# Adding the two experts' outputs of a node in one DRAM row, with the gates made earlier, in a graph layer with a top-2 mixture of experts

## The chip, the cores and the metric

The kernel runs on one core of a Trainium2 chip, in float32, as a single launch. The metric is the device time in microseconds (us) of that launch, the median of several runs.

## The reference

A graph convolution, a mixture of 64 experts of which each node uses two, a batch norm over all nodes, and a residual with a layer norm. There are N = 12,500 nodes of D = 256 values, and 212,500 edges, sorted by destination; H = 512 and CAP = 1024.

```python
h = feats * rsqrt(deg_out)[:, None]
m = segment_sum(h[src], dst) * rsqrt(deg_in)[:, None]
x = (m @ W_gc + b_gc) + (feats @ W_res + b_res)

logits = x @ Wg + bg                       # [N, 64]
vals, idx = top_k(logits, 2)
gates = softmax(vals, axis=-1)             # two gates per node, their sum is 1
# each expert e: h1 = gelu(rows @ w1[e] + b1[e]); out = h1 @ w2[e] + b2[e]
core = zeros(N, D).at[tok].add(gate * out) # the two outputs of a node, weighted
y = x + core
y = (y - mean(y, 0)) * rsqrt(var(y, 0) + 1e-5) * gamma + beta
result = layernorm(feats + y)
```

## The kernel before

P = 128 is the partition count; the nodes are NT = 98 tiles of 128 (the last one short), NP = 98 x 128 = 12,544. E = 64 experts have RPE blocks of 128 slots each, NSLOT in all. `V`, `S`, `T`, `GP` and `nc.sync` are VectorE (DVE), ScalarE (ACT), TensorE (PE), GpSimd (POOL) and SyncE (SP). The stages follow each other in time.

**Degree count.** Degrees of sources are counted by DVE while `h_d` (the scaled features) is made. Beside it SP writes zeros to all of `z_d`, in pieces of 256 KB.

**Edge and node stage.** `row(c)` gathers 128 source rows from `h_d` with an indirect DMA on POOL (L729) into a ring of 6 x 4 rows and multiplies them on PE with a one-hot matrix of their destinations; 1584 such rows are worked through. The order of all instructions here is written out by hand (`manual_schedule`): each step of the side work calls `later(t, f)`, which puts the next step LAG = 11 rows further on, and the loop over `c` takes the steps that are due. So one engine's step and the next engine's step that needs its result lie 11 rows apart. `own` issues 118 loads of 64 KB on SP here. When all edges of a pair of node tiles are summed, `nodes(t0, n, t)` runs for that pair: `square_root` (ACT) and `scales` for the degree, `scale`, `turn_x`, `turned`, `dense` (x and the 64 logits into one accumulation), then `best`: DVE adds the bias, takes the two largest logits and their places, SP writes the x rows to `x2_d` (L951), DVE keeps the difference of the two logits in `less` (L956), and `keep` copies x to `acc2`, which stays in SBUF. `count`, `ranks`, `codes`, `entries` and `enter` number each node's place within its two experts and enter it in the table `tab` by products on PE. The last three groups of tiles have no edges left beside them, so their chains run one after the other: the tail.

**Slot table.** `tab` holds per slot P * (1 + tile of the node) + row, with P * NT more for a second choice, or 0 where the slot is free. A few DVE operations (L1149 to L1164) turn it into `slot[:, 0]`, the row of `x2_d` to gather, and `slot[:, 1]`, the row of `z_d` to write: first choices to rows 0 to NP - 1, second choices to NP and on, free slots outside of it.

**Experts.** The 64 experts are taken in the order of their counts, largest first, in parts of up to four blocks (`parts`, 83 of them, 241 blocks, 28,352 slots for 25,000 rows). For each part in turn the program has `hidden` (PE and Gelu on ACT), `begin` of the part three further on (for a new expert: its table columns, and 1 MB of weights by SP, L1217 to L1219, three buffers; then `gather`, one indirect DMA per block on POOL, L1229, 16 buffers `xg`), `turn` of the next part (PE transposes and a DVE copy), and `outputs`: per block four products into `yp`, L1278 on DVE adds the bias into `yo` (six buffers), and L1279 scatters 128 rows to `z_d` on POOL. All those scatters are declared free of dependences among each other (group "places"), since each row is given once.

**End, first pass.** The gates are made from `less` (an Exp). For each of twelve loads of eight tiles, and some short ones, SP loads both halves of `z_d` (L1387, 1 MB each, two buffers of both), ACT multiplies the second choices by their gate, tile by tile (L1390), DVE multiplies the first choices and adds them to `acc2`, tile by tile (L1394), and one DVE addition per load adds the second ones (L1399). PE then transposes each tile (L1410), DVE takes the batch norm's statistics from PSUM (L1415), and ACT copies the transposed tiles back (L1417).

**End, second pass.** The batch norm is applied, x is added, and the layer norm is made and written, load by load. The x loads stand behind the z loads on SP.

Of the kernel before, what the change touches and what calls it, by code (L numbers as in the profile page):

```python
# [8 lines left out]
F32 = mybir.dt.float32  # L9
F16 = mybir.dt.float16  # L10
BF16 = mybir.dt.bfloat16
I32 = mybir.dt.int32
# [7 lines left out]
P = 128  # L20
# [81 lines left out]
def gnn_moe_kernel(  # L102
# [25 lines left out]
    x2_d = dram.tile([N, D], F32, name="x2_d")  # L128
    late_d = dram.tile([P, LATE], F32, name="late_d")
    z_d = dram.tile([2 * NP, D], F32, name="z_d")  # L130
# [55 lines left out]
    less = const.tile([P, NT], F32)  # L186
    V.memset(less, 0.0)

# [29 lines left out]
    tables = route.tile([P, 2, 2, NSLOT], I32)  # L218
    slot, sorted_ = tables[:, 0], tables[:, 1]
# [35 lines left out]
    with ExitStack() as stack:  # L255
# [23 lines left out]
        zeros = [(z_all[a], zero) for a in range(NT)]  # L279
# [356 lines left out]
    with ExitStack() as stack:  # L636
# [234 lines left out]
        def nodes(t0, n, t):  # L871
# [67 lines left out]
            def best(t):  # L939
                y, top, i8 = v["y"], v["top"], v["i8"]  # L940
                for i in range(n):
                    V.scalar_tensor_tensor(
                        y[:r, i], gps[i][:r], r_in[:r, t0 + i : t0 + i + 1], bias[:r],
                        op0=ALU.mult, op1=ALU.add,
                    )
                give("gp", t)
                for i in range(n):
                    V.max(top[:r, i], y[:r, i, D:])
                for i in range(n):
                    V.max_index(i8[:r, i], top[:r, i], y[:r, i, D:])  # L950
                nc.sync.dma_start(  # L951
                    x2_d[t0 * P : t0 * P + (n - 1) * P + r].rearrange("(t p) d -> p t d", p=r),
                    y[:r, :n, :D],
                )
                later(t, keep)
                V.tensor_sub(less[:r, t0 : t0 + n], top[:r, :n, 1], top[:r, :n, 0])  # L956
                ix = of("ix", [P, 2, 2])
                V.tensor_copy(ix[:r, :n], i8[:r, :n, 0:2])
                o1 = of("o1", [P, 2, E], BF16)
                both = of("both", [P, 2, E], BF16)  # L960
                for j in range(n):
                    V.tensor_scalar(
                        o1[:r, j], lane_b[:r, :E], ix[:r, j, 0:1], None, op0=ALU.is_equal
                    )
                    V.scalar_tensor_tensor(
                        both[:r, j], lane_b[:r, :E], ix[:r, j, 1:2], o1[:r, j],
                        op0=ALU.is_equal, op1=ALU.add,
                    )
                of("rk", [P, 2, 2])
                take("pp", t, count)  # L970

# [156 lines left out]
        with tc.manual_schedule(engines={  # L1128
# [20 lines left out]
        code = one.tile([P, NSLOT], F32)  # L1149
        V.tensor_copy(code, tab)  # L1150
        second = one.tile([P, NSLOT], F32)
        V.tensor_single_scalar(second, code, P * (NT + 1) - 0.5, op=ALU.is_gt)
        free = one.tile([P, NSLOT], F32)
        V.tensor_scalar(free, code, 0.0, OUTSIDE, op0=ALU.is_equal, op1=ALU.mult)
        node = one.tile([P, NSLOT], F32)
        V.scalar_tensor_tensor(
            node, second, float(-NP), code, op0=ALU.mult, op1=ALU.add
        )
        V.tensor_scalar(node, node, float(-P), 0.0, op0=ALU.add, op1=ALU.max)
        V.tensor_copy(slot[:, 0], node)  # L1160
        V.tensor_add(node, node, free)
        V.scalar_tensor_tensor(
            slot[:, 1], second, float(NP), node, op0=ALU.mult, op1=ALU.add
        )  # L1164
# [44 lines left out]
    with ExitStack() as stack:  # L1209
        wp = stack.enter_context(tc.tile_pool(name="w", bufs=3))  # L1210
        two = stack.enter_context(tc.tile_pool(name="x_two", bufs=2))
# [12 lines left out]
        def gather(at, n):  # L1224

            xg = []
            for k in range(n):
                g = two.tile([P, D], F32, name="xg", bufs=16)
                GP.indirect_dma_start(  # L1229
                    out=g,  # L1230
                    out_offset=None,
                    in_=x2_d,
                    in_offset=bass.IndirectOffsetOnAxis(ap=at[:, 0, k : k + 1], axis=0),
                )
                xg.append(g)
            return xg
# [30 lines left out]
        def outputs(w, bb, at, h1, m, group):  # L1267
            w2 = w[:, 2 * H : 2 * H + 4 * D].rearrange("p (c d) -> p c d", d=D)
            for k in range(-(-m // P)):
                r = min(P, m - k * P)  # L1270
                yp = ps2.tile([P, D], F32, name="yp")
                for j in range(4):
# [5 lines left out]
                V.tensor_add(yo[:r], yp[:r], bb[:r])  # L1278
                st = GP.indirect_dma_start(  # L1279
# [6 lines left out]
                    bounds_check=2 * NP - 1,  # L1286
                    oob_is_err=False,
                )
                if group:
                    tc.declare_no_dep(st.ins, group=group, reason="each row is given once")  # L1290
                    tc.add_to_no_dep_group(group, st.ins)
# [14 lines left out]
        def begin(q):  # L1306
            i, b, m = parts[q]
            if b == 0:
# [20 lines left out]
                )  # L1329
                given[i] = load(regs[i % REGS])  # L1330
# [5 lines left out]

        for q in range(AHEAD):
            begin(q)
        xT = turn(xg.pop(0))
        for q, (i, b, m) in enumerate(parts):  # L1340
            h1 = hidden(given[i][0], xT, m)
            if q + AHEAD < len(parts):
                begin(q + AHEAD)
            if q + 1 < len(parts):
                xT = turn(xg.pop(q + 1))
            outputs(*given[i], table(q), h1, m, "places")


        with tc.If(nc.values_load(over_n[0:1, 0:1]) > 0):
            with tc.For_i(0, E, 1) as e:  # L1350
                w, bb = load(e)
                at = two.tile([P, 2, RPE], I32, name="at")
                V.tensor_copy(at, slot[:, :, bass.ds(e * RPE, RPE)])
                for b in range(0, RPE, 4):
                    ab = at[:, :, b : b + 4]
                    outputs(w, bb, ab, hidden(w, turn(gather(ab, 4)), 4 * P), 4 * P, None)


    with ExitStack() as stack:
# [4 lines left out]
        zq = zq_stack.enter_context(tc.tile_pool(name="f_z", bufs=2))  # L1364
# [9 lines left out]
        gate = one.tile([P, 2, NT], F32)  # L1374
        S.activation(gate[:, 1], less, AF.Exp)
        V.tensor_scalar_add(gate[:, 0], gate[:, 1], 1.0)
        V.reciprocal(gate[:, 0], gate[:, 0])
        V.tensor_mul(gate[:, 1], gate[:, 1], gate[:, 0])


        stat = one.tile([P, 2, 25, 6], F32)
        z3 = [z_d[k * NP : (k + 1) * NP].rearrange("(t p) d -> p t d", p=P) for k in range(2)]
        for t0, n in LOADS:
            r = rows(t0)
            zt = zq.tile([P, 2, 8, D], F32, name="zt")
            for k in range(2):
                nc.sync.dma_start(zt[:r, k, :n], z3[k][:r, t0 : t0 + n])  # L1387
            for i in range(n):
                t = t0 + i
                S.activation(  # L1390
                    zt[:r, 1, i], zt[:r, 1, i], AF.Copy, scale=gate[:r, 1, t : t + 1]
                )
                y = acc2[:r, :, t * P : (t + 1) * P]
                V.scalar_tensor_tensor(  # L1394
                    y, zt[:r, 0, i].rearrange("p (h d) -> p h d", h=2),
                    gate[:r, 0, t : t + 1], y, op0=ALU.mult, op1=ALU.add,
                )
            y = acc2[:r, :, t0 * P : (t0 + n) * P].rearrange("p h (t d) -> p t h d", d=P)
            V.tensor_add(y, y, zt[:r, 1, :n].rearrange("p t (h d) -> p t h d", h=2))  # L1399
# [133 lines left out]
```

## Time and profile before

| | |
|---|---|
| median of three runs | 3382.77 us (3381.10 to 3382.91) |
| the profiled execution | 3381.99 us, span 3380.1 us |
| degree count | 0 to 260 us |
| edge and node stage | 260 to 2242 us |
| its tail and the slot table | 2242 to 2312 us |
| experts | 2312 to 3168 us |
| first pass of the end | 3168 to 3285 us |
| second pass | 3285 to 3380 us |

The stages are read off the trace: where the gathers of the edges begin and end, where PE begins to be busy without a break, where the first load of `z_d` is issued, where the last statistic is done. In the lines of the profile a group is named by its line in the kernel (L729), its engine, its operation, the tiles "out<-in", and its count; then come the busy time, the mean duration of one in ns, and the idle time of the engine just before them with what ended most of it ("<-DMA zt<-z_d": a transfer). "issue" is idle time in which the engine waited for nothing that the profile shows. The granted clock is the share of TensorE's full clock that was granted.

### The profile page before, as it was taken

The numbers are of one execution on the slowest core, as the hardware profiler recorded it, in microseconds if no ns is written. First come the engines' busy times: TensorE is split into PE (matmuls) and PEld (weight loads), VectorE is DVE, ScalarE is ACT, GpSimd is POOL, SyncE is SP. The second block draws the span as 40 slices with busy tenths as digits, with TensorE's granted clock in tenths as the row PEclk, the third lists the DMA queues.
The fourth block names the chain that finished last, engine by engine and source line by source line (L and its number), as shares of the span: only waits on it lengthen the run. The fifth ranks groups of instructions, "written<-read, shape, count | busy, mean of one in ns | idle before, by whom it ended". The sixth has DMA issues, their size and how long they took to land. (4 is left out here: it accounts for less than half of the span.)

```text
span 3380.1 us, 37103 instructions
## 1 busy us (share of the span) xinstructions
PE 2658.2 (79%) x11121; PEld 1756.8 (52%) x11121; DVE 1620.7 (48%) x6071; ACT 732.6 (22%) x2054; POOL 2001.5 (59%) x2088
## 2 busy tenths in 40 slices
PE   5828777777787777777778777867999999999644
PEld 4613344444454444444444444544777766778533
DVE  9986334545545544544454455653122222222498
ACT  8960100000011000010000101111222211222368
POOL 0027777777777777777777777735555555554100
PEclk8866778988878888998888898978999999999865
DMA  9553444444444444444444444423334444556667
GB/s 351 191 165 105 154 118 127 130 125 123 128 130 126 125 127 125 127 129 122 126 125 129 128 124 130 133 73 128 123 121 137 138 146 157 182 179 198 222 217 242
DMA packets 256999, 497.38 MB, mean 147 GB/s; under 512 B 44571, under 2 KB 168985, under 8 KB 248474
## 3 DMA queue, kind: packets, MB, share of 16 engines
q0 software_dynamic: 98800, 264.95, 27.1%
q1 hardware_dynamic: 144696, 217.20, 19.5%
q10 hardware_dynamic: 13298, 12.80, 1.3%
q8 instruction: 91, 1.49, 0.2%
q14 instruction: 114, 0.93, 0.1%
HBM read 401.41 MB, written 96.79 MB: 147 GB/s over the span
## 5 line engine op out<-in xcount | busy, mean ns | idle before, releaser
L729 POOL DMA_INDIRECT ring<-h_d,src_col x1584 | 1511.0, 954 | 495.3 <-issue 425.3
L743 PE MATMUL p<-ring,o 128*128 128x258 f32 x3168 | 1179.6, 482 | 481.8 <-DMA ring<-h_d,src_col 400.1
L743 PEld LDWEIGHTS p<-ring,o 128*128 128x128 f32 x3168 | 603.5, 222 | 976.5 <-DMA ring<-h_d,src_col 647.2
L721 DVE TENSOR_SCALAR o<-lane,rel 128x128 f32<-128x128 f32 x1584 | 384.3, 302 | 591.5 <-PE p L743 591.3
L1273 PE MATMUL yp<-w,h 128*128 128x256 f32 (+3 forms) x1928 | 432.9, 380 | 0.0
L1229 POOL DMA_INDIRECT xg<-x_d,tables x241 | 233.0, 967 | 335.8 <-PE xtp L1244 219.3
L1257 PE MATMUL hp<-xT,w 128*128 128x384 f32 (+11 forms) x1328 | 399.5, 454 | 1.4 <-DVE xT L1248 1.4
L1273 PEld LDWEIGHTS yp<-w,h 128*128 128x128 f32 (+3 forms) x1928 | 341.9, 182 | 64.4 <-issue 7.3
L1261 ACT ACTIVATE h<-hp,w 128x384 f32<-128x384 f32 (+11 forms) x332 | 180.9, 545 | 670.0 <-PE hp L1257 669.1
L776 ACT COPY s<-p 128x258 f32<-128x258 f32 x132 | 49.3, 373 | 1241.6 <-PE p L743 1241.5
L1257 PEld LDWEIGHTS hp<-xT,w 128*128 128x128 f32 x1328 | 248.4, 191 | 131.2 <-issue 56.9
L1279 POOL DMA_INDIRECT z_d<-yo,tables x241 | 238.1, 988 | 121.9 <-DVE yo L1278 65.0
L1248 DVE COPY xT<-xtp 128x768 f32<-128x768 f32 (+2 forms) x83 | 77.4, 932 | 405.6 <-PE xtp L1244 405.6
L1278 DVE TENSOR_TENSOR yo<-yp,bb 128x256 f32<-128x256 f32 (+3 forms) x241 | 102.1, 423 | 276.2 <-PE yp L1273 270.7
L435 ACT ACTIVATE s_lo<-lane_b,nb 128x128 bf16<-128x128 bf16 x581 | 171.0, 387 | 4.4 <-DVE lo_end L426 1.8
L1043 PE MATMUL tab<-at,vals 128*128 128x512 bf16 x392 | 139.7, 447 | 11.6 <-DVE vals L1031 11.6
L583 POOL MEMSET acc<- 128x1792 f32 x10 | 17.5, 1754 | 213.7 <-DMA h_d<-acc 213.7
L928 PE MATMUL bank<-wcat,acc 128*128 128x320 f32 x392 | 137.1, 477 | 0.0
L841 DVE TENSOR_TENSOR acc<-q,acc 128x256 f32 x132 | 55.8, 423 | 159.7 <-PE q L818 109.2
L933 PE MATMUL bank<-wcat,xT 128*128 128x320 f32 x392 | 127.7, 450 | 0.0
L738 ACT CAST ring<-mark 128x4 f32<-128x4 bf16 x354 | 57.8, 197 | 259.6 <-issue 259.6
L928 PEld LDWEIGHTS bank<-wcat,acc 128*128 128x128 f32 x392 | 83.5, 213 | 32.4 <-issue 7.3
(276 smaller groups left out, 2553.3 us busy)
## 6 DMA issues: line engine op xcount, KB each, us to landing
w<-in_wpack SPq DMA_DIRECT2D x64, 1026.0 KB
ring<-h_d,src_col POOLq DMA_INDIRECT x1584
z_d<-tables SPq DMA_DIRECT2D x98, 256.0 KB
zt<-z_d SPq DMA_DIRECT2D x24, 1024.0 KB
tables<-h_d SPq DMA_DIRECT2D x118, 128.0 KB
xt<-in_x ACTq DMA_DIRECT2D x48, 256.0 KB
x_d<-y SPq DMA_DIRECT2D x48, 256.0 KB
z<-in_x SPq DMA_DIRECT2D x12, 1024.0 KB
```

The costliest lines, as they stand in the source:

```text
L435: S.activation(s_lo[:, i], lane_b, AF.Sign, bias=nb[:, k, i : i + 1])
L721: o_last[u] = V.tensor_scalar(o_of[u][:, j], lane, rel[:, c : c + 1], None, op0=ALU.is_equal)
L729: i = GP.indirect_dma_start(out=r[:, k, :D], out_offset=None, in_=h_d, in_offset=bass.IndirectOffsetOnAxis(ap=src_col[:, c : c + 1], axis=0),)
L743: i = T.matmul(p_of[g], o_of[v][:, n], r[:, k], start=j == 0, stop=j == GR - 1)
L928: T.matmul(gps[i][:r], acc2[:, k, a : a + r], wcat[:, k], start=k == 0, stop=False,)
L933: T.matmul(gps[i][:r], v["xT"][:, i, k, :r], wcat[:, 2 + k], start=False, stop=k == 1,)
L1043: T.matmul(tab, vals[:r, m], at[:r], start=t0 + i + k + m == 0, stop=t0 + i == NT - 1 and k + m == 2,)
L1229: GP.indirect_dma_start(out=g, out_offset=None, in_=x2_d, in_offset=bass.IndirectOffsetOnAxis(ap=at[:, 0, k : k + 1], axis=0),)
L1257: T.matmul(hp[:, :m], w1[:, c, j * P : (j + 1) * P], xT[:, c, :m], start=c == 0, stop=c == 1,)
L1261: S.activation(h1[:, j, :m], hp[:, :m], AF.Gelu, bias=w[:, 2 * H + 4 * D + j : 2 * H + 4 * D + j + 1],)
L1273: T.matmul(yp[:r], h1[:, j, k * P : k * P + r], w2[:, j], start=j == 0, stop=j == 3,)
L1279: st = GP.indirect_dma_start(out=z_d, out_offset=bass.IndirectOffsetOnAxis(ap=at[:r, 1, k : k + 1], axis=0), in_=yo[:r], in_offset=None, b ...
```

## The change

`z_d` has one row per node instead of two. The scatter of L1279 adds to it (`compute_op=ALU.add`), and what it adds is already multiplied by the gate. The gates are made in the node stage, right where the logits are compared, and are written as two further columns of `x2_d`; the expert stage's gather brings them with the row, and a flag per slot (`snd`) tells which of the two is meant. The columns are the first gate and the second minus the first, so that the gate of a slot is `first + flag * difference`.

[...]No node has the same expert twice, so the scatters of one expert are declared independent of each other (group `expert{i}`); the first scatter of each expert has a dependence on those of the expert before. Free slots no longer go outside the bounds: each goes to a row of its own behind the nodes' rows (N + block * 128 + partition), and the bounds check is gone.

In the end stage one load per eight tiles and one addition are left of the loads, products and additions there.

```diff
-    x2_d = dram.tile([N, D], F32, name="x2_d")
+    x2_d = dram.tile([N, D2], F32, name="x2_d")
-    z_d = dram.tile([2 * NP, D], F32, name="z_d")
+    z_d = dram.tile([NP + 4 * 2 * P, D], F32, name="z_d")
...
-        zeros = [(z_all[a], zero) for a in range(NT)]
+        zeros = [(z_all[a], zero) for a in range(NT // 2 + 4)]
...
@@ best(t)
-                nc.sync.dma_start(
-                    x2_d[...].rearrange("(t p) d -> p t d", p=r),
-                    y[:r, :n, :D],
-                )
                 later(t, keep)
-                V.tensor_sub(less[:r, t0 : t0 + n], top[:r, :n, 1], top[:r, :n, 0])
+                V.tensor_sub(of("less", [P, 2])[:r, :n], top[:r, :n, 1], top[:r, :n, 0])
+                later(t, exponential)
...
+            def exponential(t):
+                S.activation(v["less"][:r, :n], v["less"][:r, :n], AF.Exp)
+                later(t, gates)
+
+            def gates(t):
+                e, y = v["less"][:r, :n], v["y"]
+                p = of("gate", [P, 2])[:r, :n]
+                V.tensor_scalar_add(p, e, 1.0)
+                V.reciprocal(p, p)
+                V.tensor_copy(y[:r, :n, D], p)
+                V.scalar_tensor_tensor(
+                    y[:r, :n, D + 1], e, -1.0, p, op0=ALU.add, op1=ALU.mult
+                )
+                nc.sync.dma_start(
+                    x2_d[...].rearrange("(t p) d -> p t d", p=r),
+                    y[:r, :n, :D2],
+                )
...
@@ slot table
+        spread = one.tile([P, NSLOT], I32)
+        GP.iota(spread, pattern=[[0, E], [P, RPE]], base=N, channel_multiplier=1)
+        V.tensor_single_scalar(second, tab, P * (NT + 1) - 0.5, op=ALU.is_gt)
+        V.scalar_tensor_tensor(node, second, float(-NP), tab, op0=ALU.mult, op1=ALU.add)
+        V.tensor_scalar(slot[:, 0], node, float(-P), 0.0, op0=ALU.add, op1=ALU.max)
+        V.tensor_copy(snd, second)
+        V.tensor_single_scalar(free, tab, 0.0, op=ALU.is_equal)
+        V.tensor_tensor(free, free, spread, op=ALU.mult)
+        V.tensor_tensor(slot[:, 1], free, slot[:, 0], op=ALU.add)
...
@@ experts
-                g = two.tile([P, D], F32, name="xg", bufs=16)
+                g = two.tile([P, D2], F32, name="xg", bufs=16)
...
+        def gates_of(xg, second):
+            gate = two.tile([P, 4], F32, name="gate", bufs=4)
+            for k, g in enumerate(xg):
+                V.scalar_tensor_tensor(
+                    gate[:, k : k + 1], second[:, k : k + 1], g[:, D + 1 :], g[:, D : D + 1],
+                    op0=ALU.mult, op1=ALU.add,
+                )
+            return gate
...
                 V.tensor_add(yo[:r], yp[:r], bb[:r])
+                V.tensor_scalar_mul(yo[:r], yo[:r], gate[:r, k : k + 1])
                 st = GP.indirect_dma_start(
...
-                    bounds_check=2 * NP - 1,
-                    oob_is_err=False,
+                    compute_op=ALU.add,
                 )
...
+        def turned(q):
+            i, b, m = parts[q]
+            gate[q] = gates_of(xg[q], snd_sorted[:, i * RPE + b : i * RPE + b + 4])
+            return turn(xg.pop(q))
...
-            outputs(*given[i], table(q), h1, m, "places")
+            outputs(*given[i], table(q), gate.pop(q), h1, m, f"expert{i}")
...
@@ first pass of the end
-        zq = zq_stack.enter_context(tc.tile_pool(name="f_z", bufs=2))
+        zq = zq_stack.enter_context(tc.tile_pool(name="f_z", bufs=4))
...
-            zt = zq.tile([P, 2, 8, D], F32, name="zt")
-            for k in range(2):
-                nc.sync.dma_start(zt[:r, k, :n], z3[k][:r, t0 : t0 + n])
-            for i in range(n):
-                t = t0 + i
-                S.activation(
-                    zt[:r, 1, i], zt[:r, 1, i], AF.Copy, scale=gate[:r, 1, t : t + 1]
-                )
-                y = acc2[:r, :, t * P : (t + 1) * P]
-                V.scalar_tensor_tensor(
-                    y, zt[:r, 0, i].rearrange("p (h d) -> p h d", h=2),
-                    gate[:r, 0, t : t + 1], y, op0=ALU.mult, op1=ALU.add,
-                )
+            zt = zq.tile([P, 8, D], F32, name="zt")
+            nc.sync.dma_start(zt[:r, :n], z3[:r, t0 : t0 + n])
             y = acc2[:r, :, t0 * P : (t0 + n) * P].rearrange("p h (t d) -> p t h d", d=P)
-            V.tensor_add(y, y, zt[:r, 1, :n].rearrange("p t (h d) -> p t h d", h=2))
+            V.tensor_add(y, y, zt[:r, :n].rearrange("p t (h d) -> p t h d", h=2))
```

## The prediction

> **What bounds the kernel now.** I read the busy times by stage first, then the costliest groups, then the last two stages line by line.[...]
>
> ```profile
> 260.00:2242.00 1982.00, 1536.58 (x5196) 912.30 (x5196) 984.79 (x4654) 185.77 (x732) 1499.10 (x1572) 0.86 0.44 127
> 2242.00:2312.00 70.00, 32.88 (x89) 16.95 (x90) 36.44 (x222) 5.64 (x15) 12.61 (x14) 0.62 0.24 84
> 2312.00:3168.00 856.00, 855.28 (x3726) 642.58 (x3724) 180.07 (x338) 182.16 (x333) 457.57 (x468) 1.00 0.48 150
> 3168.00:3285.00 117.00, 41.62 (x196) 37.34 (x196) 102.04 (x183) 68.91 (x153) 0.91 (x1) 0.64 0.84 265
> 3285.00:3380.00 95.00, 45.54 (x196) 35.02 (x196) 78.10 (x330) 78.76 (x140) 0.00 (x0) 0.55 0.65 215
> ```
>
> The columns are the length, busy PE, PEld, DVE, ACT and POOL, the granted clock, the DMA share and GB/s. In the experts PE is busy 855 of 856 us, so only what stops PE counts there. In the first pass DVE is busy 102 of 117 us and the DMA engines 84%: both are near their limit. Before 2242 no engine is full, and the groups say who sets the pace:
>
> ```profile
> L729 POOL DMA_INDIRECT ring<-h_d,src_col x1584 | 1511.0, 954 | 495.3 <-issue 425.3
> L1229 POOL DMA_INDIRECT xg<-x_d,tables x241 | 233.0, 967 | 335.8 <-PE xtp L1244 219.3
> L1279 POOL DMA_INDIRECT z_d<-yo,tables x241 | 238.1, 988 | 121.9 <-DVE yo L1278 65.0
> ```
>
> L729's idle time is almost all "issue", the 0.3 us between two gathers: POOL paces the edges at 1.25 us a gather, and ACT (186 of 1982 us) and DVE (985) have room. The first pass, by lines:
>
> ```profile
> L1390 ACT ACTIVATE zt<-zt,gate 128x256 f32<-128x256 f32 x98 | 42.2, 501 | 36.3 <-DMA zt<-z_d 19.6 <-issue 16.7
> L1394 DVE SCALAR_TENSOR_TENSOR acc<-zt,gate,acc 128x256 f32<-128x256 f32 x98 | 41.3, 478 | 10.0 <-DMA zt<-z_d 9.8
> L1415 DVE BATCH_NORM_STATS2 stat<-q 128x6 f32<-128x512 f32 (+1 forms) x50 | 32.2, 678 | 0.8 <-PE q L1410 0.8
> L1399 DVE TENSOR_TENSOR acc<-acc,zt 128x2048 f32<-128x2048 f32 (+2 forms) x14 | 28.2, 2016 | 0.8 <-ACT zt L1390 0.5
> ```
>
> **The change, part by part.**
>
> *First pass.* L1394 (98 x 0.478 = 41.3 us of DVE) and L1390 (42.2 of ACT) go, and z halves from 25.7 to 12.8 MB. The new DVE program takes two blocks of eight tiles at a time: two additions of 2.29 us (the full form of L1399 in the timeline), then eight statistics of 0.68: 10.0 us. PE's 32 transposes (3.65 us for 16, from the timeline) start after the first addition, so the last statistic ends at 2.3 + 0.1 + 7.3 + 0.7 = 10.4. I take 10.4. DMA needs 12.8 MB of z and 5.1 of x, at 265 to 350 GB/s 51 to 68 us, in step with 62; four buffers keep it ahead. The first z data was there at 3177.4. The first pair ends at 3187.9 (its second load comes about 3.2 us later), five more at 3239.9, the short tiles and the aggregates take 3.3: 3243 against 3281 now. **-38**, with -31 (DMA at the low rate) to -44. The second pass starts earlier and is the same.
>
> *Scatter.* 241 scatters that add. POOL's row now is 0.99 us; of 32 rows it took 0.88 and of 128 rows 1.00, so little of it goes by the row. Below: 0.99. Above: twice, 2.0, if every row needs twice the descriptors. I take 1.1, near the row: 241 x 0.1 = 26 us on a POOL that is busy 458 of 856 (with 0.3 a row between, about 600). Hidden. Bounds checks go, so free slots write too: 28,352 rows instead of 25,000, over 16 DMA engines at 48% share. Hidden.
>
> *The new wait.* The first scatter of an expert now waits until the last one of the expert before has landed. Behind it on POOL stand this expert's other scatters and the gathers of the part four further on, needed three parts later. Six yo buffers are between it and PE. The order repeats, here with 224 tokens:
>
> ```profile
> 3126.70 0.33 SPq L1219 DMA_DIRECT2D w<-in_wpack  x1
> 3127.30 0.92 POOL L1279 DMA_INDIRECT z_d<-yo,tables  x1 [0.74 <-DVE yo L1278]
> 3132.50 0.99 POOL L1279 DMA_INDIRECT z_d<-yo,tables  x1 [4.28 <-DVE yo L1278]
> ```
>
> The DMA view (packets, MB, busy share) shows when the scatter of 3127.30 landed. From 3128.3 to 3131.3 only the weight load moved:
>
> ```profile
> q1 hardware_dynamic: 187, 0.96, 84.7%
> ```
>
> The scatter's queue, q0, came in the two us after that, up to 3133.4:
>
> ```profile
> q1 hardware_dynamic: 84, 0.09, 11.4%
> q0 software_dynamic: 48, 0.08, 10.0%
> ```
>
> So landing takes up to 6.1 us from the start beside a weight load; the quiet one of 3125.58 had moved its 0.13 MB by 3127.7, 2.1 us. The Trainium skill ("DMA: Bandwidth & Descriptors", Anatomy of one DMA) puts such a transfer at 2.0 us plus bytes over 436 GB/s, 2.3 us for 128 KB, and warns that with HBM as the target the receipt can take surprisingly long. By 2.3 us the wait is nothing, as the gap is 5.2; by the trace's 6.1 it is 0.9 us. I go by the trace. The adding itself: below +0.4 (each packet took 0.18 us for four rows, two a DMA engine, read twice), above +2.1 (the whole quiet landing again); I take 0.5. A delayed first scatter moves the second only if landing exceeds 6.92 - 1.3 = 5.6 us, with 6.92 the period of this expert. At 6.1 + 0.5 that is 1 us in five such experts at worst, and the last three have no weight load and catch up. **+1**, with 0 to +20. The last landing and the multiplication before it: **+0.8**.
>
> *DVE beside PE.* A product per block (128x256; the 128x512 TENSOR_SCALAR row is 0.42, so about 0.25) and a gate column (0.16): 100 us on a DVE busy 180 of 856; yp is freed before the product. 0.
>
> *Gates in the node stage.* Four DVE operations of 0.16 us per pair: 32 us, under POOL's pace. Sqrt and Exp now alternate on ACT, with 92 more table loads:
>
> ```profile
> L193 ACT ACT_TABLE_LOAD x2 | 2.6, 1283 | 0.0
> ```
>
> 118 us on an ACT busy 186 of 1982; a PE delayed by 1.3 us is made up, since POOL fills 24 ring rows ahead. The skill ("ScalarE: Activation LUTs", What ACT_TABLE_LOAD costs) adds a 1.38 us drain to each switch, 2.66 in all. Here Sqrt or Exp followed its load within 0.02 us, so I take 1.28. It matters in the tail: after the copy that ends at 2258.1 a load and Exp end at 2259.6, before DVE gets to the gates at 2260.4 and the next scaling at 2260.5. With 2.66 it would be late, about 1.5 us over the tail. By the trace 0. DVE's four operations are in line in the tail, three times 0.75: **+2.2**. The write of x2 rows (49 DMAs, now 1032 B a row) moves two lags, some 27 us, down SP's queue; behind it stand the 118 loads of own rows, needed as late again, and at the end the first weight loads, which wait till 2294 while the last write issues at about 2285. 0, above +3.
>
> *Other.* The slot table: seven operations for eight, same 4.4 us; iota on POOL 0.55, beside it. 45 zero writes of 256 KB fewer in a stage where DVE is busy 239 of 260 us: 0, with -3 to 0.
>
> Sum: -38 + 1 + 0.8 + 2.2 = **-34**. The profiled execution took 3381.99 (span 3380.1), 0.8 under the median 3382.77. So 3348 as profiled, **3349** as a median.
>
> **Rivals.**
> 1. *The wait becomes the pace (slower).* In backlog an expert of n blocks takes (n-1) x 1.3 + landing. With landing at 9 us the excess over the period (from the weight issues: 6.92 at 224 tokens, 7.35 at 256, about 6.5 at 192, 10.0 at 288, 10.5 at 320 and 352) is 17 + 18 + 8 + 6 + 12 = 60 us: 3408. It decides from 8 us on, where it is 32 and cancels the gain. For: 6.1 us without the addition. Against: landing is tied to the end of the weight load, so a later start waits less.
> 2. *An adding scatter costs POOL far more (slower).* POOL needs 241 x 1.27 = 306 us for gathers; with a scatter row of 2.1 + 0.3 us it fills 856 + 34. At 2.5 us: 306 + 675 = 981, 125 over: 3474. Against: rows matter little now.
> 3. *The pass stays bound elsewhere:* late z data or slower transposes, 80 us instead of 66: 3363.
>
> **How the numbers follow.** Mine 0.60 (3338 to 3360), rival 3 0.10, both faster. Rival 1 near its balance 0.05, counted as no change; beyond it 0.12; rival 2 0.13. A measurement can tell 0.2%, 6.8 us. Faster 0.70, same 0.05, slower 0.25. The range runs from the low end of the pass to a landing just over 9 us, 3335 to 3420; most of rival 2 lies outside.
>
> **What would show it.** Right: the first pass near 66 us with DVE over 90% busy; PE still at 100% in the experts; scatter rows under 1.3 us; waits of POOL's first scatter on DMA of about 1 us an expert; the edge stage as long as now; the tail 2 us longer. Wrong: PE waiting for xg or yp, POOL rows over 2 us, landings over 8 us.

## The result, and the profile after

The changed kernel took 3354.96 us (median of four runs, 3353.21 to 3357.62) against 3382.16 for the kernel before: 27.2 us less, a ratio of 0.992 with a 95% interval of 0.9909 to 0.9932. The forecast was 3349, 6 us lower. The profiled execution took 3356.17 us, its span is 3354.4. Spans are compared below, 25.7 us apart.

The stages of the changed kernel, from the view by windows (length, busy PE, PEld, DVE, ACT and POOL, the granted clock, the DMA share and GB/s). The borders are those where the same things happen as before: edges, tail, experts up to the last product, hand-over up to the first addition, first pass, second pass.

```profile
245.00:2254.00 2009.00, 1581.47 (x5204) 943.98 (x5205) 1022.20 (x4879) 313.78 (x868) 1524.24 (x1584) 0.83 0.44 126
2254.00:2320.00 66.00, 29.16 (x98) 16.05 (x96) 35.38 (x219) 11.32 (x21) 9.94 (x11) 0.67 0.22 75
2320.00:3181.00 861.00, 859.13 (x3729) 643.48 (x3730) 314.70 (x896) 182.50 (x333) 600.42 (x471) 1.00 0.67 154
3181.00:3195.50 14.50, 0.39 (x2) 0.00 (x0) 0.76 (x2) 0.00 (x0) 2.98 (x2) 0.63 0.44 110
3195.50:3258.50 63.00, 35.52 (x196) 33.38 (x196) 60.52 (x82) 30.20 (x52) 0.00 (x0) 0.72 0.83 266
3258.50:3354.00 95.50, 46.04 (x196) 35.06 (x196) 78.08 (x331) 79.05 (x140) 0.00 (x0) 0.54 0.65 214
```

In order, with the lengths before read off the trace in the same way:

| stage | before | after | difference | forecast |
|---|---|---|---|---|
| up to the first gather | 244.5 | 244.8 | +0.3 | 0 |
| edges, first to last gather | 1995.6 | 2009.1 | **+13.5** | 0 |
| last edge gather to first product of the experts | 68.1 | 66.2 | -1.9 | +2.2 |
| experts | 859.2 | 861.3 | +2.1 | +1 |
| last product to first addition of the end | 10.2 | 14.2 | +4.0 | +0.8 |
| first pass and its aggregates | 107.3 | 62.9 | **-44.4** | -38 |
| second pass | 95.4 | 95.8 | +0.4 | 0 |

So the gain of the first pass was larger than forecast, and almost a third of it (13.5 of 44.4 us) was lost in a stage for which the forecast had no cost at all. The groups that answer to those shown of before (busy time, mean ns, idle time before them and what ended it):

```profile
L727 POOL DMA_INDIRECT ring<-h_d,src_col x1584 | 1524.5, 962 | 495.4 <-issue 429.7 <-PE p L741 43.0 <-DMA h_d<-acc 10.8
L1241 POOL DMA_INDIRECT xg<-x_d,tables x241 | 236.4, 981 | 199.8 <-PE xtp L1256 97.4 <-DVE snd_sorted L1352 50.0 <-PE yp L1295 24.4
L1302 POOL DMA_INDIRECT z_d<-yo,tables x241 | 376.1, 1561 | 115.5 <-issue 60.3 <-DVE yo L1301 21.7 <-DVE gate L1283 17.7
L1422 DVE TENSOR_TENSOR acc<-acc,zt 128x2048 f32<-128x2048 f32 (+2 forms) x14 | 27.7, 2012 | 14.1 <-DMA zt<-z_d 14.1
L1438 DVE BATCH_NORM_STATS2 stat<-q 128x6 f32<-128x512 f32 (+1 forms) x50 | 30.3, 668 | 0.4 <-PE q L1433 0.2
```

The edge gather's mean went from 954 to 962 ns with its idle time unchanged; the scatter's from 988 to 1561. In the first pass of the end, the additions and the statistics are all that DVE has: 58 of 60.5 us.

**The first pass** in the timeline of DVE and of PE:

```profile
3234.07 4.48 DVE L1422 TENSOR_TENSOR acc<-acc,zt 128x2048 f32<-128x2048 f32 x2
3238.47 4.88 DVE L1438 BATCH_NORM_STATS2 stat<-q 128x6 f32<-128x512 f32 x8
3243.26 4.47 DVE L1422 TENSOR_TENSOR acc<-acc,zt 128x2048 f32<-128x2048 f32 x2
```

```profile
3236.49 5.19 PE L1433 MATMUL q<-ident,acc 128*128 128x128 f32 x32 [3.23 <-DVE acc L1422]
```

This pair of blocks takes 9.2 us (3234.07 to 3243.26), with DVE never idle; the six pairs take 9.2 to 10.0, 9.5 in the mean. Each addition starts 2.19 us after the one before it and each statistic 0.60 us after the one before, although their rows last 2.28 and 0.68 us: the rows overlap. PE turned this pair's 32 tiles in 5.19 us (the six pairs: 5.2 to 6.5), beginning under the second addition; at the 3.65 us for 16 of the kernel before it would have been 7.3. The view by windows shows why (columns as above; matmul counts in brackets behind PE's busy time):

```profile
3236.40:3239.20 2.80, 2.71 (x13) 2.74 (x14) 2.80 (x3) 0.01 (x1) 0.00 (x0) 0.50 0.94 284
3239.30:3241.50 2.20, 2.20 (x20) 2.02 (x19) 2.20 (x5) 2.17 (x4) 0.00 (x0) 0.98 1.04 363
```

At a granted clock of 0.50 one transpose follows another every 0.213 us, at 0.98 every 0.109 us. The 3.65 us for 16 in the kernel before fell wholly into a stretch at 0.50; here each pair has part of its transposes at the higher clock.

**The hand-over** in the timeline of POOL and SP:

```profile
3178.46 1.43 POOL L1302 DMA_INDIRECT z_d<-yo,tables  x1 [0.30 <-issue]
3182.99 1.56 POOL L1302 DMA_INDIRECT z_d<-yo,tables  x1 [3.10 <-DVEq L1382]
3184.85 1.42 POOL L1302 DMA_INDIRECT z_d<-yo,tables  x1 [0.30 <-issue]
```

```profile
3189.83 5.50 SPq L1420 DMA_DIRECT2D zt<-z_d  x4
```

The last two scatters belong to the last expert. Its first row of outputs was multiplied by its gate at 3180.37 (L1301), its last at 3182.22; yet the first scatter starts at 3182.99. The wait is put down to "DVEq L1382", which had long been done: it is the other semaphore of this scatter, the landing of the expert before (that scatter, of 3178.46, landed at 3182.27). The second scatter stands behind it on POOL, 2.6 us after its data. Then come 1.4 us of its own row and 3.6 to the z load.

**The experts** show one wait of PE, and it is none of those that the forecast spoke of:

```profile
PE yp L1295 <- DVE yo L1300: 1.8, 1, 1.8
```

It falls at 2335, in the first part. DVE's timeline there:

```profile
2327.27 0.22 DVE L1283 SCALAR_TENSOR_TENSOR gate<-snd_sorted,xg 128x1 f32<-128x1 f32 x1 [1.04 <-DMA xg<-x_d,tables]
2329.30 0.22 DVE L1283 SCALAR_TENSOR_TENSOR gate<-snd_sorted,xg 128x1 f32<-128x1 f32 x1 [0.77 <-DMA xg<-x_d,tables]
2330.92 0.22 DVE L1283 SCALAR_TENSOR_TENSOR gate<-snd_sorted,xg 128x1 f32<-128x1 f32 x1 [1.22 <-DMA xg<-x_d,tables]
```

The gates of a part are read out of the gathered rows, so DVE now waits for gathers, and at the start of the stage POOL delivers one only every 1.26 us. Behind these waits on DVE stands the table work (L1348, and L1352, which is new: it copies the flags) and behind that the bias addition that frees `yp`: it starts at 2335.09, when PE has waited for the buffer since 2333.8.

```profile
2331.56 0.17 DVE L1352 CAST snd_sorted<-snd 128x8 f32 x1
```

Ten such copies, each 0.11 us of DVE's time, stand between the last gate and that addition, 1.1 us in all. How much of the 1.8 us is theirs and how much is the gates' wait was not taken apart.

### The profile page after: what moved, and what is told of

Read it like the earlier page. It is cut to its first block, busy times and chain, and to the rows that moved or that the text cites. A ratio compares the mean times of both kernels' runs of the same rounds, so it can differ in the third digit from the quotient of the medians.

```text
span 3354.4 us, 37394 instructions
## 1 busy us (share of the span) xinstructions
PE 2688.7 (80%) x11121; PEld 1781.7 (53%) x11121; DVE 1738.0 (52%) x6714; ACT 828.1 (25%) x2097; POOL 2157.1 (64%) x2089
## 5 line engine op out<-in xcount | busy, mean ns | idle before, releaser
L727 POOL DMA_INDIRECT ring<-h_d,src_col x1584 | 1524.5, 962 | 495.4 <-issue 429.7
L741 PE MATMUL p<-ring,o 128*128 128x258 f32 x3168 | 1204.4, 492 | 452.4 <-DMA ring<-h_d,src_col 362.6
L741 PEld LDWEIGHTS p<-ring,o 128*128 128x128 f32 x3168 | 623.8, 228 | 947.8 <-DMA ring<-h_d,src_col 621.2
L1302 POOL DMA_INDIRECT z_d<-yo,tables x241 | 376.1, 1561 | 115.5 <-issue 60.3
L1057 PE MATMUL tab<-at,vals 128*128 128x512 bf16 x392 | 149.2, 473 | 14.6 <-DVE vals L1045 14.6
```

The costliest lines, as they stand in the source:

```text
L727: i = GP.indirect_dma_start(out=r[:, k, :D], out_offset=None, in_=h_d, in_offset=bass.IndirectOffsetOnAxis(ap=src_col[:, c : c + 1], axis=0),)
L741: i = T.matmul(p_of[g], o_of[v][:, n], r[:, k], start=j == 0, stop=j == GR - 1)
L1057: T.matmul(tab, vals[:r, m], at[:r], start=t0 + i + k + m == 0, stop=t0 + i == NT - 1 and k + m == 2,)
L1302: st = GP.indirect_dma_start(out=z_d, out_offset=bass.IndirectOffsetOnAxis(ap=at[:r, 1, k : k + 1], axis=0), in_=yo[:r], in_offset=None, c ...
```

## The experiments

The theory after the result: the first pass gained 44 us, the hand-over lost 4 by the wait between experts and the slower landing of an adding scatter, and 13 us were lost to a gather that takes 8 ns longer. The last is the puzzle: the instruction is unchanged, and the first gather runs 2 ms before the first adding scatter. Single instructions of L727 in the view by source (minimum, median, maximum in ns); the kernel before has 942/946/1439:

```profile
L727 POOL DMA_INDIRECT ring<-h_d,src_col x1584: 949/954/1442, 244.8 to 2252.9; - x198
```

1583 steps of 8 ns are 12.7 of the 13.5 us. Each ratio below is to the kernel before on the same chip; two versions of the changed kernel are compared by these ratios and by their profiles.

**e1: the kernel before, once more.** No edit.

> The kernel before, unchanged, profiled a second time. In the changed kernel each gather of the edge stage took 8 ns more (954 for 946 ns, the most common value), 13 us over 1584 of them. Theory A (something in the changed program does it): here 946 ns again, and the gathers run from first to last in 1995 us. Theory B (it is the execution or the chip's state): the row differs from 946 by some ns.

One run of 3382.29 us.

```profile
L729 POOL DMA_INDIRECT ring<-h_d,src_col x1584: 942/946/1439, 245.0 to 2240.4; - x198
```

The row is the same to the ns, so this one repeat shows none of the 8 ns: it speaks for theory A.

**e2: scatters that write.**

```diff
                     in_offset=None,
-                    compute_op=ALU.add,
                 )
```

> The changed kernel with scatters that write instead of add (this leaves out the sum of a node's two outputs; the waits between experts stay). It prices the addition. Theory: the scatter's POOL row falls from 1.56 to about 1.0 us, its landing from 3.4 us (quiet) to 2.3, the wait at the hand-over to the end stage shrinks by 2 to 3 us, experts 1 us; total 3 to 4 us below the changed kernel. Rival 1: an adding transfer somewhere in the program also makes every gather 8 ns longer: then the edge stage is 13 us shorter as well and the total 16 us below. Rival 2: the addition costs nothing on the path: same time as the changed kernel within 2 us.

3340.12 us (3337.16 to 3342.90), ratio 0.9878 (0.9862 to 0.9894): 15 us below the changed kernel, as the first rival said.

```profile
L727 POOL DMA_INDIRECT ring<-h_d,src_col x1584: 942/946/1438, 245.2 to 2238.6; - x198
L1302 POOL DMA_INDIRECT z_d<-yo,tables x241 | 234.3, 972 | 132.8 <-DVE yo L1301 52.1 <-issue 30.2 <-DVE gate L1283 27.6
```

The edge stage is 14.7 us shorter than in the changed kernel, the hand-over 2.6 us (11.6 for 14.2). What the addition costs a scatter is read from the same two profiles: POOL's row 1561 ns for 972, the landing by the view of issues in the expert stage 4.6 us in the median for 3.1 (the traces have it for 124 and 75 of the 241 scatters; the same adding scatters in e8 have 5.3), and packets of its queue there:

```profile
q0 software_dynamic: 22768, 60.90, 23.0%
```

```profile
q0 software_dynamic: 43776, 60.90, 40.2%
```

The first line is the writing kernel, the second the changed one: the same 60.9 MB, but 21,008 packets more, 87 for each scatter. The experts take 861.4 us in this kernel too, with the same wait of PE (1.7 us, and 1.2 in e4; e3 and the kernel before have none), so their 2 us are not the addition's.

**e3: the gates made in the node stage, alone.** The kernel before with `exponential` and `gates` as in the change and x rows of 258 columns; `less`, slots, scatters and end as before.

```diff
-                nc.sync.dma_start(x2_d[...], y[:r, :n, :D])
                 later(t, keep)
                 V.tensor_sub(less[:r, t0 : t0 + n], top[:r, :n, 1], top[:r, :n, 0])
+                later(t, exponential)
...
-                g = two.tile([P, D], F32, name="xg", bufs=16)
+                g = two.tile([P, D2], F32, name="xg", bufs=16)
```

> The kernel before with the gates also made in the node stage and written and gathered as two more columns (258 wide), and nothing else changed: slots, scatters and end as before. It prices the node part alone. Theory: edge stage as long as before (within 2 us), tail within 2 us, so 3382 within 3 us. Rival 1: the node part, with its 92 table loads and its later and wider writes, is what lengthens the gathers: 954 ns, +13 us, 3396. Rival 2: it costs in the tail: +2 to +5 us.

3381.46 us against 3381.15, ratio 1.0000 (0.9990 to 1.0009); gathers of 946 ns. The theory held: 92 table loads, the later write and the wider rows cost nothing that can be measured. Its tail, from the last edge gather to the first of the experts, is 56.1 us against 55.4 and 54.9 in the two profiles of before, less than the 2.2 us forecast.

**e4: no wait between experts.** Two rows per node again, each given once, still adding; bounds check as before, and the end loads the first choices alone. (The lines for the zeros and the slot numbers are not shown.)

```diff
-    z_d = dram.tile([NP + 4 * 2 * P, D], F32, name="z_d")
+    z_d = dram.tile([2 * NP, D], F32, name="z_d")
...
-            outputs(..., f"expert{i}")
+            outputs(..., "places")
```

> The changed kernel with two rows per node in the scattered array again, still adding, each row given once: all scatters in one group, so no wait between experts; free slots go out of bounds as in the kernel before (the end stage loads the first choices alone, which leaves out the second ones). It prices the wait between experts. Theory: the wait costs 1.8 us of PE and about 3 us at the hand-over, where the last expert's first scatter waited 3.1 us: total 4 to 5 us below the changed kernel. Rival 1: the wait was covered by other things and the hand-over is set by landing alone: within 1 us of the changed kernel. Rival 2: the wait also held back gathers behind it on POOL: over 8 us below.

3356.43 us (3356.22 to 3356.94), ratio 0.9926 (0.9909 to 0.9943): no different from the changed kernel. The wait shows at the hand-over alone, which is 11.8 us for 14.2: the last scatter starts 0.3 us after its data instead of 2.6; the experts take 861.2 us with it or without it. The 2.4 us were given back by a longer edge stage and tail (2009.8 and 55.5 us for 2009.1 and 54.2), which is within what single profiles differ by. So the price of 4 to 5 us was too high. Rival 1 is nearest in its number, but not in its reason: the wait does lengthen the hand-over.

**e5: an adding scatter that never runs.** In the kernel before, in the fallback branch.

```diff
                     oob_is_err=False,
+                    **({} if group else {"compute_op": ALU.add}),
```

> The kernel before, with the adding scatter only in the fallback branch that these inputs never enter; every scatter that runs writes as before. Theory A (that an adding indirect transfer is in the program at all makes every indirect transfer of POOL longer): gathers of 953 to 954 ns for 946, edge stage +13 us, 3394. Theory B (adding transfers must run to matter): 946 ns and 3381, no change.

3380.11 us against 3379.52 (0.9992 to 1.0011), gathers of 946 ns: that such a transfer stands in the program does nothing.

**e6: only the last expert adds.**

```diff
-                    compute_op=ALU.add,
+                    **({"compute_op": ALU.add} if group == f"expert{E - 1}" else {}),
```

> The changed kernel in which only the last expert's two scatters add, and all others write (this leaves out the sum of most nodes' two outputs). Theory A: the gathers, which are over 900 us before the first addition, take 953 to 954 ns, edge stage 2009 us, total 3353 to 3355 (the plain one's 3340 plus 13). Theory B (something in proportion to the adding transfers, 241 of them): at most 0.1 ns more per gather, 3340.

3341.04 us (3338.95 to 3341.54), gathers of 946 ns: two adding scatters that run don't lengthen the gathers either.

**e7: every scatter waits for the one before.**

```diff
             for k in range(-(-m // P)):
                 r = min(P, m - k * P)
+                if group:
+                    group = f"scatter{len(seen)}"
+                    seen.append(k)
```

> The changed kernel with each scatter waiting for the landing of the one before it, 241 waits for 63. It tests the formula of the first rival (an expert of n blocks takes n landings when all of them wait). Landing by the trace of the changed kernel: 4.5 us median, 3.4 quiet. Theory (wait = landing + about 0.4 us of signalling, as it is in the changed trace): experts 241 x 4.9 = 1180 us for 861, total about 3675. Rival: landings are long only where a weight load is beside them, and become 3.4 when POOL is slower: 241 x 3.8 = 916, total about 3410. Rival 2: hidden as now: 3355.

3749.5 us, 395 above the changed kernel and 75 above the theory's 3675; the rivals were far off. From the first scatter to the last, POOL:

```profile
3414.01 1.58 POOL L1305 DMA_INDIRECT z_d<-yo,tables  x1 [3.01 <-DVE yo L1303]
3418.64 1.36 POOL L1305 DMA_INDIRECT z_d<-yo,tables  x1 [3.05 <-DVE yo L1303]
```

```profile
z_d<-yo,tables POOLq DMA_INDIRECT x241, 3.9
```

4.63 us from start to start, where the landing is 3.9 us in the median. (Again DVE is named, whose output had long been ready.) This landing is read at the semaphore; from there to the next start it takes 0.8 us in the median, and 0.7 to 0.8 in the changed kernel's trace, not 0.4. (The last completion packet of the queue ends earlier, 3.5 us from the start and 1.1 before the next one.) Over the stage it is 1243 us from the first scatter (2334.2) to the last (3577.4), 5.2 for each of 240 steps.

**e8: two buffers for z.** `bufs=2` for 4 in the pool of `zt`.

> The changed kernel with two buffers for the z loads in the first pass, as before, for four. Theory (DVE sets the pass's 59.5 us, and a load of 1 MB takes 3 to 4 us of the 9.5 that DVE needs for two): the pair of additions frees both buffers at once and the next pair has 4.9 us of statistics to arrive in, 2 MB need about 6: +1 to +2 us per pair, 5 to 10 us in all. Rival: DMA is early enough with two: same time within 2 us.

3354.20 us (3352.29 to 3356.97), ratio 0.9927 (0.9910 to 0.9943), first pass 60.2 us to the last statistic for 59.5: the same, so the rival. The additions come first in the pair and free both buffers; after the first pair DVE waits for z data twice, 0.8 us in all.

The last four runs fell on chips that grant less clock in the edge stage (0.74 for 0.83) and where the kernel before takes 3681 us; they are compared with that.

**e9: 125 of 241 scatters add** (experts 21 to 63; the expectation has 110, a miscount: 125 rows of POOL show the longer time of an adding scatter).

> The changed kernel in which the scatters of experts 21 to 63 add (110 of the 241) and those before write (this leaves out part of the sums). Two adding scatters (the run with the last expert alone) left the gathers at 946 ns, 241 gave 953 to 954. Theory A (the gathers lengthen in proportion to the adding transfers): 949 to 950 ns, edge stage 2000 us, total about 3346. Theory B (a threshold in their number): 946 or 953 to 954 and nothing between, total about 3340 or 3354.

3644.54 us against 3681.46, ratio 0.9901 (0.9881 to 0.9921).

```profile
L727 POOL DMA_INDIRECT ring<-h_d,src_col x1584: 947/953/1451, 245.0 to 2529.8; - x198
```

Not in proportion: 125 give what 241 give. That looked like a threshold.

**e10: as many packets, no addition.**

```diff
-                    compute_op=ALU.add,
...
+        for k in range(438):
+            gather(table(0), 1)
```

> The changed kernel with scatters that write (leaving out the sum) and 438 more gathers of x rows behind the last scatter, whose result is not used. The adding scatters raised the packets of the software queue from 98,800 to 119,808; 438 gathers of 48 packets do the same without an addition. Theory A (the length of the queue's work in a program sets the gather's row): edge gathers of 953 to 954 ns. Theory B (it is the addition): 946 ns. The 438 gathers take 438 x 1.25 = 548 us at the end, so the total is 3340 + 550 = 3890 in either case, 13 us more under A.

4212.58 us; with the 300 us that this chip adds to the kernel before, 4190 was to be expected. The software queue has 119,824 packets, and the edge gathers take 946 ns: the length of the queue's work is not it.

**e11: five of the twelve additions of the first pass on POOL.**

```diff
+            on = GP if t0 in (8, 24, 40, 56, 72) else V
-            V.tensor_add(y, y, ...)
+            on.tensor_add(y, y, ...)
```

> The changed kernel with five of the twelve large additions of the first pass on POOL, which is idle there, instead of DVE. Theory (DVE sets the pass): DVE's work for a pair falls from 9.4 to 7.1 us, POOL's addition runs beside the other one; if it takes up to about 5 us the five pairs save about 2.1 us each: 10 us, 3345. Rival 1: POOL's addition takes over 7 us (no row of the trace has a POOL addition), the pair waits for it: no gain or up to 20 us lost. Rival 2: DVE's additions slow down beside POOL's: half of the gain.

3648.72 us against 3681.46, ratio 0.9911 (0.9895 to 0.9928). The first pass is 62.9 us to the last statistic, 3.3 longer than the 59.6 of e12: no gain.

```profile
L727 POOL DMA_INDIRECT ring<-h_d,src_col x1584: 940/946/1445, 245.8 to 2533.0; - x198
```

```profile
3502.82 5.10 POOL L1423 TENSOR_TENSOR acc<-acc,zt 128x2048 f32<-128x2048 f32 x1 [1.44 <-DMA zt<-z_d]
```

```profile
3503.45 6.61 DVE L1423 TENSOR_TENSOR acc<-acc,zt 128x2048 f32<-128x2048 f32 x1
```

POOL's additions take 4.5 to 6.2 us, and the three of DVE's that begin beside one take 4.7 to 6.6 instead of 2.3: each ends 2.1 to 2.2 us after POOL's, as if it had begun with POOL's end. The Trainium skill ("SBUF — State Buffer", Who interferes with whom) says just this: a DVE instruction with two SBUF inputs contends with a GpSimd instruction that reads SBUF. Rival 2, and worse than it said. The run also upset the other question: all 241 scatters add here, and the edge gathers take 946 ns.

**e12: the changed kernel, once more.** No edit.

> The changed kernel, unchanged, a second time. Five programs with all or many adding scatters had edge gathers of 953 to 954 ns; the one with five additions on POOL had all 241 adding scatters and 946 ns, so the addition alone does not set it. Theory A (it goes by the program as it lies in memory, the same at every loading): 953 to 954 ns again. Theory B (it falls out anew at each loading or on each chip): 946 ns is possible; on a chip where the edges wait for POOL, the total would then be near 3341 instead of 3355.

3645.49 us against 3680.64, ratio 0.9903 (0.9886 to 0.9919), 35.1 us less.

```profile
L727 POOL DMA_INDIRECT ring<-h_d,src_col x1584: 950/957/1451, 245.2 to 2530.0; - x198
```

957 ns at a second loading, near the 954 of the first: this one repeat speaks for theory A. But here it costs nothing: from the first gather to the last 2285.7 us, and in e10, with 946 ns, 2285.9. Where PE is held back (granted clock 0.74), POOL's gather no longer sets the pace.

**What is shown of the 8 ns.** Every profile has one of two values, 946 or 953 to 957 ns, for nearly all edge gathers from the first on. Three chips had a profile of either value. Each of the two kernels that were profiled twice kept to its value (946 and 946, 954 and 957). Taking the addition off the changed kernel brought 946, with 14.7 us of edge stage; but adding scatters are not enough (e11), nor is their number (e9 against e11), nor the number of packets (e10).

The traces show one thing more: the longer value ends within the launch, at the first scatter that adds. These are the gathers of x rows before and after it, in e9, where the first 116 scatters write, and in the changed kernel (minimum, median, maximum in ns):

```profile
L1241 POOL DMA_INDIRECT xg<-x_d,tables x140: 949/968/1007, 2589.7 to 3040.7; - x140
L1241 POOL DMA_INDIRECT xg<-x_d,tables x101: 942/981/1032, 3051.5 to 3405.8; - x101
```

```profile
L1241 POOL DMA_INDIRECT xg<-x_d,tables x24: 949/954/994, 2308.1 to 2337.1; - x24
L1241 POOL DMA_INDIRECT xg<-x_d,tables x217: 942/982/1063, 2346.6 to 3118.4; - x109
```

The first two gathers behind a scatter mostly take longer, in every program, and hide it in these medians. The third and later ones have medians of 953 to 957 ns up to the first adding scatter and 946 to 949 behind it, in all six profiles with the longer value; in e9, 116 writing scatters did not end it. So the longer value is there before any addition of the launch, and an addition takes it away. What in a program brings it about stays open. None of the kernels tried is both complete and faster than the changed one.

## Why the prediction was right or wrong

**Direction and mechanism: right.** The first pass paid for everything, and it is DVE's, as foreseen: 58 of its 60.5 us are additions and statistics. The forecast's time was 6 us low on a move of 27, and that it was so near is in part luck: against the forecast the first pass came out 6.4 us shorter and the tail 4.1, the edge stage 13.5 longer, the hand-over 3.2 and the experts 1.1. Of its signs of being right, three did not come (scatter rows under 1.3 us, an edge stage as long as before, a longer tail); of its signs of being wrong, PE's wait for `yp` came once, for 1.8 us.

**First pass, -38 forecast, -44 measured.** The mis-sized term is the 10.4 us per pair; 9.5 were measured in the mean. It has two errors. DVE's own work was put at 10.0 us by adding up the rows' durations, which overlap: it was 9.2. And PE's 32 transposes were put at 7.3 us into a chain behind the first addition, at the rate of a stretch with a granted clock of 0.50; they took 5.2 to 6.5. The fear for DMA (51 to 68 us) was not borne out, and the four buffers were not needed (e8). Rival 3, 80 us, is out.

**Edge stage, 0 forecast, +13.5 measured.** This is the step that failed: the forecast put the stage at nothing because it costed only waits and added instructions there, and none of those did cost anything (e3). That an unchanged instruction might come out 8 ns longer was not considered, nor what it would weigh: 1584 of them set the pace, so 1 ns is 1.6 us. On a chip where they don't set it (e12) the gain was 35 us.

**The new wait, +1 forecast.** Landing is 4.6 us in the median and 3.4 to 7.9 in the range, against 5.6 from which a delay was to show; 36 of the 124 landings in the trace are above that. The wait is there: against its data and POOL's row before it, the first scatter of an expert starts up to 3.6 us late, 38 us in all (6 in e4, which has no such wait), 31 of them in the last 14 experts. e4 shows that in the experts it costs PE nothing all the same. The addition's part of a landing was taken at 0.5 us; by e2 it is 1.5 in the median (3.1 to 4.6), in the upper half of its bounds of 0.4 and 2.1. Going by the trace rather than by the 2.3 us that the formula of the Trainium skill ("DMA: Bandwidth & Descriptors", Anatomy of one DMA) gives for 128 KB was right: no landing of an adding scatter in the traces was under 2.8 (e7).

**Rival 1 (the wait becomes the pace).** It needed a landing of 8 us. The mechanism is real, as e7 shows, where it cost 395 us; and with the 0.8 us between a landing and the next start, which the rival left out, the longest landings of 7.9 pass its balance of 8. They are too rare to count: 7 of 124 are over 7 us. (Its terms add up to 61 us, not 60.)

**Rival 2 (the row of the adding scatter).** 1.1 us was taken, 1.56 measured, within the bounds of 0.99 and 2.0, with 87 further packets per scatter. Little of the increase goes by the row: 32 rows take 1.34 us for 0.88 before, 128 rows 1.59 for 1.00. (For a row of 2.1 us the rival's sum is 884 us, 28 over the stage, not 34.) It was costed at nothing with POOL as cover, and this held: POOL is busy 600 of 861 us, and PE never waited for a scatter or a gather.

**The hand-over, +0.8 forecast, +4.0 measured.** The wait at the last expert (2.6 us before the last scatter's start, 0.3 in e4) was missed, because the forecast let the last three experts "catch up": they have no weight load, but the last one's first scatter still waits for a landing. The addition brings its part: without it the hand-over is 11.6 us (e2), without the wait 11.8 (e4), with both 14.2. The two parts can't be added up, since a later landing also lengthens the wait.

**The experts, 0 for DVE's work, +2.1 measured.** The product (0.37 us for the 0.25 estimated) and the gate (0.215 for 0.16) are hidden. But neither the gate's wait for the gathered rows nor the copies of the flags were named, and at the start of the stage nothing covers them: 1.8 us of PE.

**The tail, +2.2 forecast; 0.7 to 1.2 in e3.** In the changed kernel it is shorter than before, with a slot table of seven operations for eight. The table loads cost nothing:

```profile
L968 ACT ACT_TABLE_LOAD x47 | 60.3, 1283 | 1.2 <-DVE less L950 0.3
L884 ACT ACT_TABLE_LOAD x46 | 59.0, 1283 | 0.8
```

The 93 loads have 2.0 us of idle time before them in all, and behind them Sqrt or Exp starts within 0.02 us wherever its data is there. A drain of 1.38 us at each, as the Trainium skill has it ("ScalarE: Activation LUTs", What ACT_TABLE_LOAD costs), would show as 128 us. Taking the row's 1.28 was right.

## What to carry to other kernels

Where one instruction that is issued 1584 times sets the pace, its duration is a term of the sum even if the change doesn't touch it, and the range should hold a per cent of it. Work of one engine is better read from start to start than added up from the rows. An adding scatter is worth its price where POOL has room: what it costs is a longer row and a longer landing, so look for the place where a landing stands alone on the path, at the end of the stage. And a value that moves from one engine's table into gathered data makes its reader wait for the gather: name what stands behind that reader.

## What was not expected of the hardware

- An indirect gather of 128 rows of 1 KB has one of two durations, 946 or 953 to 957 ns, for a whole edge stage. The longer one ends with the first adding scatter of the launch; what brings it about is open.
- An adding scatter takes POOL 1.56 us for 0.97 in the mean, has 87 more packets, and lands 1.5 us later in the median.
- Between the landing of one scatter and the start of the next that waits for it 0.8 us pass (1.1 from the last completion packet).
- A DVE addition of 128x2048 that begins beside one on POOL takes up to 6.61 us for 2.3.
- DVE's rows of one kind overlap: a statistic of 0.68 us is followed by the next after 0.60. Adding up durations gives too much.
